# A third place for scores in the last unit, and reciprocals by block transposes instead of through DRAM

## The chip, the cores and the metric

The kernel runs on one core of one Trainium2 chip. The metric is the time of one execution in device microseconds (us); runs of the same kernel are summed up by their median. In the profile PE is TensorE (matrix products), DVE VectorE, ACT ScalarE, POOL GpSimd and SP the engine that issues most transfers (DMAs). Each engine works through its own instructions in the order in which the program lists them.

## The reference

Four batches of 1024 tokens, 512 features, go through three layers, each behind a layer norm and added to its input: a gated self-attention, a cross-attention on a context of 384 features, and a feed-forward layer of 64 small networks. The change lies in the cross-attention of the last batch:

```python
q = (query @ Wq + bq)...; k = (key_value @ Wk + bk)...; v = (key_value @ Wv + bv)...   # 16 heads of 32
attn = jnp.einsum('bhqd,bhkd->bhqk', q, k) * scale
attn = jax.nn.softmax(attn, axis=-1)
x = jnp.einsum('bhqk,bhkd->bqhd', attn, v).reshape(B, Nq, Cq)
return x @ Wo + bo
```

The feed-forward layer takes a scalar per network from the normalized tokens (s), passes it through 16 hidden units (h = relu(s * W1 + b1)), sums them with weights (g) and maps the 64 results back to 512 features. All is in float32.

## The kernel before

The work is cut into eight units: four batches in the first phase (self-attention), then four in the second (cross-attention). A unit has two halves of 512 queries, a half four groups g of four heads, a group eight steps kt, one for each 128 keys. So a unit has 64 steps; this text counts those of the last unit from 0 to 63.

A step (`step`, in `attention`) lists, in this order: what is due ahead of it; `scores`; what is due behind them; and `finish` of the step before, that is `times`. `scores` (L578) makes the transposed scores of two pairs of heads. Each pair has a place s of two PSUM banks; the pool `mps` has two such places, used in turn. ScalarE takes the exponential of a pair into e (L583, 128x1024); e has six buffers. `times` (L624) multiplies four heads' e by the values into the one bank av. In the last unit VectorE adds the e of steps 0 to 3 and of 4 to 7 of a group (L591, tiles sets). The sums over the keys come from TensorE with a column of ones: `by_ones` (L614) for steps 0 to 3, listed two steps after kt = 3, so in steps 5, 13, 21 and so on; `add_up` (L652) for the rest, in the second step of the next group. Both write the one bank sm, and only one row of each 32.

`normalize` evicts av into the tile both (ScalarE, L641) in the step after a group's last. Then the sums go on a way through DRAM, each part listed a few steps after the one before: `add_up` evicts sm (ScalarE, L653), writes four rows to DRAM and reads them back as 128 rows of 16 (L658, L660); three steps later `divide` takes the reciprocal (L689), two reductions for a check of the range (L690, L691), writes it to DRAM (L692) and reads each head's row back onto 32 partitions (L696, four transfers, tile recb); three more steps later `multiply` (L702) divides. The group of step 63 (`closing`) is done otherwise, in `settle`: its sums are made 32 columns wide and the reciprocal is taken from PSUM.

What else goes on is woven between the steps by `run`: `beside` gives a list of parts, each with a load in matmul blocks or 0, and `run` lists after each step as many as keep the shares of load equal. In the last unit the list of a half holds, of the half before: hidden units (L880 on ScalarE, then L884 and L886 on VectorE; hid has two buffers, so the hidden unit h waits for the VectorE instruction that has read h - 2), the output projection (L87 into a single bank f; steps 6 to 13 and 38 to 45), the output of the feed-forward layer of the half before that (L897, L903; steps 14 and 15, 46 and 47), layer norm (L290 to L299, L303), rows written to and read back from DRAM (L307, L312), the addition of the bias (L844), block transposes (L318) and the feed-forward input (L859; steps 24 and 56), which needs all four transposes. The pool `mpf` has two single banks f, which only these parts use. Parts without load, such as hidden units, fall into steps without matmuls of their own. [...]

The order of instructions on each engine is the order in which the code lists them.

Of the kernel before, what the change touches and what calls it, by code (L numbers as in the profile page):

```python
# [16 lines left out]
P = 128  # L17
# [46 lines left out]
def moderate_path(tc: tile.TileContext, a: dict, out: bass.AP, flag: bass.AP):  # L64
    nc = tc.nc
    x = a["x"]
    with ExitStack() as st:
# [9 lines left out]
        p3 = enter(tc.tile_pool(name="mp3", bufs=3))  # L77
        p4 = enter(tc.tile_pool(name="mp4", bufs=4))

        def bank():  # L80
            return pf.tile([P, HALF], F32, tag="f", name="f")

        def columns(to, lhsT, rhs, **flags):

# [268 lines left out]
        def pre(u):  # L353
# [194 lines left out]
                r[k] = [f(hf) for hf in range(2)]  # L548
            return r

        def attention(u, hf):

            ph, b = order[u]
# [13 lines left out]
            def closing(g):  # L567
                return (u, hf, g) == (len(order) - 1, 1, HG - 1)

            def scores(g, kt):  # L570
                q, k = me["q", hf], me["k"]
                es = []
                for i in range(2):
                    s = ps.tile([P, 2, HALF], F32, tag="s", name="s")
                    for j in range(2):
                        r = slice((2 * i + j) * DH, (2 * i + j + 1) * DH)
                        for m in range(0, P, 64):
                            nc.tensor.matmul(  # L578
                                s[m : m + 64, j, :], lhsT=k[r, g, kt * P + m : kt * P + m + 64], rhs=q[r, g, :],
                                start=True, stop=True,  # L580
                            )
                    e = p4.tile([P, 2, HALF], F32, tag="e", name="e", bufs=6)
                    nc.scalar.activation(e, s, AF.Exp, scale=SCALE)  # L583
                    es.append(e)
                me["e", kt] = es
                if fours:
                    if kt == 4 * (kt // 4) or closing(g) and kt == NT - 1:
                        return es
                    to = me["es"] = me["sets"][2 * (kt // 4) : 2 * (kt // 4) + 2]
                    for i in range(2):  # L590
                        nc.vector.tensor_tensor(to[i], me["e", kt - 1][i] if kt % 4 == 1 else to[i], es[i], ALU.add)  # L591
                    if kt == 3:
                        after(2, lambda: by_ones(g, to, True, False), behind=True)
                    return es
                for i in range(1 if shared else 2):
                    if kt == 1:
                        me.setdefault("es", {})[i] = p1.tile([P, 2, HALF], F32, tag=f"es{i}", name="es")
                        nc.vector.tensor_tensor(me["es"][i], me["e", 0][i], es[i], ALU.add)  # L598
                    elif kt > 1:
                        nc.vector.tensor_tensor(me["es"][i], me["es"][i], es[i], ALU.add)  # L600
                if ph == 0 and kt > 0:
                    if kt == 1:
                        me["eg"] = p1.tile([P, 2, HALF], F32, tag="es1", name="eg")
                    for h in range(2):
                        eg, gate = me["eg"][:, h, :], lambda t: me["sw"][:, t, HG * g + h, 1:2]
                        if kt == 1:
                            nc.vector.tensor_scalar(eg, me["e", 0][0][:, h, :], gate(0), None, ALU.mult)
                        nc.vector.scalar_tensor_tensor(eg, es[0][:, h, :], gate(kt), eg, ALU.mult, ALU.add)  # L608
                return es

            def by_ones(g, tiles, first, last):
                width = DH if closing(g) else 1
                for j in range(HG):
                    nc.tensor.matmul(  # L614
                        sm[j * DH : j * DH + width, :], lhsT=ones.to_broadcast([P, width]) if width > 1 else ones,
                        rhs=tiles[j // 2][:, j % 2, :], start=first, stop=last,
                    )
# [20 lines left out]
            def normalize(g):  # L638
                i = (u * 2 + hf) * HG + g
                both = p1.tile([P, 3, HALF], F32, tag="both", name="both")  # L640
                nc.scalar.copy(both[:, 0, :], av)  # L641
                if shared:
                    nc.scalar.copy(both[:, 1, :], sm)
                    added = [me["es"][0][:, 0, :], me["es"][0][:, 1, :], me["eg"][:, 0, :], me["eg"][:, 1, :]]
                else:
                    added = [me["es"][h // 2][:, h % 2, :] for h in range(HG)]
                after(1, lambda: add_up(g, i, both, added), behind=True)

            def add_up(g, i, both, added):

                for j, e in enumerate(added):
                    nc.tensor.matmul(sm[j * DH : j * DH + 1, :], lhsT=ones, rhs=e, start=not fours, stop=True)  # L652
                nc.scalar.copy(both[:, 2, :], sm)  # L653

                c, s1, s2 = cs_[i % 2], sum1_d[i % 4], sum2_d[i % 4]
                rows = both.rearrange("(j r) s q -> j r s q", r=DH)
                n = len(added)
# [13 lines left out]
                after(apart(g), lambda: divide(g, i, both, c))  # L671

            def divide(g, i, both, c):
                if shared:
# [71 lines left out]
        def post(u, hf):  # L746
# [24 lines left out]
            def project(t):  # L771
                def part(cs, to=None):
                    def f():
                        assert last or me["divided", hf] >= cs[-1]
                        if cs[0] == 0:
                            res["po"] = to() if to else bank()
                            res["po", t] = res["po"]
                        if last:
                            res["po"] = res["po", t]
                        for c in cs:  # L780
                            columns(
                                res["po"], me["q", hf][:, c, ts(t, P)], me["wo", hf][:, c, :],
                                start=(c == 0), stop=(c == NC - 1),
                            )
                        if cs[-1] < NC - 1:
                            return
                        r = res[t]
                        nc.vector.tensor_tensor(r, res["po"], r, ALU.add)  # L788
                        s6 = p2.tile([P, 6], F32, tag="bnst1", name="bnst1")
                        if t == 0:  # L790
                            res["mv"] = p2.tile([P, 4, 2], F32, tag="fmv", name="fmv")
                        nc.vector.bn_stats(s6, r)
                        nc.vector.bn_aggr(res["mv"][:, t, :], s6)
                        if ph == 0:
                            r2 = p2.tile([P, D], F32, tag="r2", name="r2")
                            nc.gpsimd.tensor_tensor(r2, r, bo_bc, ALU.add)  # L796
                            nc.sync.dma_start(x1b_d[b][4 * hf + t], r2)
                    return len(cs), f
                if last:
                    return [part([0, 1, 2], (lambda: ps.tile([P, 2, HALF], F32, tag="s", name="s")[:, 0, :]) if t > 1 else None), part([3])]  # L800
                return [part([c]) for c in range(4)]
# [146 lines left out]
                done = upto  # L948
            return [out + second[done:]]

        def run(main, items):

            parts = sum(items, [])
            total = sum(c for c, _ in parts)
            done = 0
            for n, f in enumerate(main):
                f()
                while parts and (done + parts[0][0] / 2 <= total * (n + 1) / len(main) or n == len(main) - 1):
                    c, f1 = parts.pop(0)
                    if f1:  # L960
                        f1()
                    done += c
# [95 lines left out]
        for u in range(n):  # L1058
            if u == 0:
                crossing.append(True)  # L1060
            for hf in range(2):
                run(attention(u, hf), beside(u, hf))
        tail = ending[0]
        sums, divide, look = settle(n - 1, 1, HG - 1)
        late.pop(0)()
# [676 lines left out]
```

## Time and profile before

| | |
|---|---|
| median of 3 runs | 2200.36 us (2195.76 to 2202.55) |
| the profiled execution | 2200.93 us, span 2199.1 us |
| PE, DVE, ACT busy | 2162.2, 1594.5, 1233.7 us |
| last unit, steps 0 to 63 | 1928.18 to 2146 us |
| exponential of a pair (L583) | 1.02 us, 1024 in all, 128 of them in the last unit |
| addition of a pair (L591) | 1.22 us |
| recb from DRAM (L696) | 64 KB each, 252 transfers |
| mean granted TensorE clock | 0.996 |

The span runs from the first instruction to the last. A line of a timeline gives the start, the length, the engine, the line of the code, the operation with output and input, and in brackets the idle time before it with the instruction that ended it. Successive matmuls of one line are drawn together as one block; a matmul is recorded twice (x16 is eight instructions). A block that waits inside is drawn longer, and its wait isn't idle time. A line of stretches gives, after the length, the busy time of PE, of its weight loads, of DVE, ACT and POOL with the number of instructions, then the granted clock, the DMA share and GB/s. A line of waits gives who waited for whom, the sum, how often and the longest.

### The profile page before, as it was taken

The page shows a single profiled execution, that of the slowest core. Times are in us where ns is not written, and L with a number is a line of the kernel's source. Part 1 is how long each engine was busy: PE and PEld are TensorE (multiplying, and loading weights), DVE is VectorE, ACT ScalarE, POOL GpSimd, SP SyncE. Part 2 cuts the span into 40 slices and gives each one's busy share as a digit, 9 for nine tenths or more (in the row PEclk, how much of TensorE's full clock was granted, in tenths as well). Part 3 has the DMA queues.
Part 4 walks back from the last instruction along what each step waited for, and adds up shares of the span by engine and source line. Part 5 has one row for each costly group of instructions (what it writes and reads, how often), then busy time and mean ns, then how long its engine had stood idle before and what let it go on. Part 6 is the DMA issues. An engine that isn't in the chain of part 4 may idle for free.

```text
span 2199.1 us, 52499 instructions
## 1 busy us (share of the span) xinstructions
PE 2162.2 (98%) x22482; PEld 545.9 (25%) x22482; DVE 1594.5 (73%) x2550; ACT 1233.7 (56%) x1482; POOL 81.7 (4%) x118
## 2 busy tenths in 40 slices
PE   8999999999999999999999999999999999999986
PEld 3322222222222222222222222222222222222222
DVE  4478675796757957567677676877777777878776
ACT  0155545555455554555656566675757666576663
POOL 1000000030210000000000000000000000000000
PEclk9999999999999999999999999999999999999998
DMA  4412123132231221211222132322233142212131
GB/s 141 130 62 55 63 95 106 29 88 66 97 104 32 82 69 47 69 56 42 70 85 90 45 90 67 79 73 56 69 84 112 50 103 69 64 36 76 62 88 41
DMA packets 152715, 161.63 MB, mean 73 GB/s; under 512 B 45628, under 2 KB 91324, under 8 KB 151320
## 3 DMA queue, kind: packets, MB, share of 16 engines
q1 hardware_dynamic: 148480, 156.08, 24.5%
q8 instruction: 178, 2.92, 0.6%
q0 software_dynamic: 2144, 0.98, 0.3%
q10 hardware_dynamic: 1848, 1.12, 0.2%
q14 instruction: 65, 0.53, 0.1%
HBM read 115.38 MB, written 42.71 MB: 72 GB/s over the span
## 4 chain that ended last, share of the span: by engine, by line
PE 92%; DVE 4%; issue 1%; DMA 1%; ACT 1%; SPq 0%; DVEq 0%; ACTq 0%
PE f L87 36%; PE s L578 25%; PE av L624 21%; PE sm L632 5%; PE sm L652 3%; DVE sets L591 1%; PE f L859 1%; ACT e L583 1%; DMA rec_d<-rec 0%; PE f L897 0%; DVE g L886 0%; PE sm L614 0%; DVE res L903 0%; PE f L471 0%; DMA recb<-rec_d 0%
## 5 line engine op out<-in xcount | busy, mean ns | idle before, releaser
L583 ACT ACTIVATE e<-s 128x1024 f32<-128x1024 f32 x1024 | 993.4, 1022 | 702.2 <-PE s L578 505.1
L600 DVE TENSOR_TENSOR es<-es,e 128x1024 f32<-128x1024 f32 x480 | 576.8, 1228 | 211.3 <-ACT e L583 209.6
L578 PE MATMUL s<-q,k 32*64 32x512 f32 x8192 | 610.6, 613 | 2.4 <-ACT e L583 0.9
L624 PE MATMUL av<-e,v 128*32 128x512 f32 x4096 | 544.8, 603 | 0.0
L87 PE MATMUL f<-xT,w 128*32 128x512 f32 x2816 | 333.7, 592 | 1.1 <-issue 1.1
L608 DVE SCALAR_TENSOR_TENSOR eg<-e,sw,eg 128x512 f32<-128x512 f32 x448 | 318.6, 747 | 2.3
L578 PEld LDWEIGHTS s<-q,k 32*64 32x64 f32 x8192 | 133.6, 129 | 448.7 <-ACT e L583 246.2
L87 PE MATMUL f<-w,q 128*32 128x512 f32 x1984 | 238.1, 592 | 0.0
L598 DVE TENSOR_TENSOR es<-e 128x1024 f32<-128x1024 f32 x80 | 95.8, 1223 | 192.9 <-ACT e L583 166.3
L624 PEld LDWEIGHTS av<-e,v 128*32 128x32 f32 x4096 | 88.0, 108 | 402.4 <-issue 399.1
L87 PEld LDWEIGHTS f<-xT,w 128*32 128x32 f32 x2816 | 92.1, 110 | 211.8 <-issue 206.4
L632 PE MATMUL sm<-e,sw 128*2 128x512 f32 x1024 | 133.3, 592 | 0.0
L87 PE MATMUL f<-w,xT 128*32 128x512 f32 x896 | 106.0, 592 | 0.6 <-DVE q L284 0.6
L87 PEld LDWEIGHTS f<-w,q 128*32 128x32 f32 x1984 | 64.5, 110 | 149.3 <-issue 142.8
L87 PE MATMUL f<-w,ctxT 128*32 128x512 f32 x768 | 92.6, 592 | 0.0
L87 PE MATMUL f<-ctxT,w 128*32 128x512 f32 x768 | 92.3, 592 | 0.0
L880 ACT ACTIVATE hid<-sT,units 128x256 f32<-128x256 f32 x128 | 76.6, 605 | 26.7 <-DVE g L886 22.9
L591 DVE TENSOR_TENSOR sets<-sets,e 128x1024 f32<-128x1024 f32 x62 | 73.1, 1221 | 9.3 <-ACT e L583 9.2
L796 POOL TENSOR_TENSOR r<-res,bo_bc 128x512 f32<-128x512 f32 x32 | 40.9, 1279 | 1041.9 <-DVE res L788 796.0
L886 DVE SCALAR_TENSOR_TENSOR g<-hid,units,g 128x256 f32<-128x256 f32 x120 | 57.6, 480 | 12.9 <-ACT hid L880 7.7
L591 DVE TENSOR_TENSOR sets<-e 128x1024 f32<-128x1024 f32 x32 | 37.8, 1221 | 30.6 <-ACT e L583 30.6
L652 PE MATMUL sm<-es,ones 128*1 128x512 f32 x320 | 57.8, 591 | 0.0
(243 smaller groups left out, 1108.1 us busy)
## 6 DMA issues: line engine op xcount, KB each, us to landing
recb<-rec_d SPq DMA_DIRECT2D x252, 64.0 KB
xT<-rows_d SPq DMA_DIRECT2D x60, 256.0 KB
rows_d<-r SPq DMA_DIRECT2D x60, 256.0 KB
w<-in_xattn_Wo SPq DMA_DIRECT2D x9, 1024.0 KB
w<-wout_d SPq DMA_DIRECT2D x8, 1024.0 KB
res<-in_x SPq DMA_DIRECT2D x32, 256.0 KB
x1b_d<-r SPq DMA_DIRECT2D x32, 256.0 KB
res<-x1b_d SPq DMA_DIRECT2D x32, 256.0 KB
```

Of the source, the lines that this page charges most:

```text
L87: nc.tensor.matmul(to[r], lhsT=lhsT[:, j, :] if len(lhsT.shape) == 3 else lhsT[:, r], rhs=rhs, **flags)
L578: nc.tensor.matmul(s[m : m + 64, j, :], lhsT=k[r, g, kt * P + m : kt * P + m + 64], rhs=q[r, g, :], start=True, stop=True,)
L583: nc.scalar.activation(e, s, AF.Exp, scale=SCALE)
L591: nc.vector.tensor_tensor(to[i], me["e", kt - 1][i] if kt % 4 == 1 else to[i], es[i], ALU.add)
L598: nc.vector.tensor_tensor(me["es"][i], me["e", 0][i], es[i], ALU.add)
L600: nc.vector.tensor_tensor(me["es"][i], me["es"][i], es[i], ALU.add)
L608: nc.vector.scalar_tensor_tensor(eg, es[0][:, h, :], gate(kt), eg, ALU.mult, ALU.add)
L624: nc.tensor.matmul(av[r, :], lhsT=me["v"][:, kt, HG * g + h, :], rhs=es[h // 2][:, h % 2, :], start=(kt == 0), stop=(kt == NT - 1),)
L632: nc.tensor.matmul(sm[j * DH : j * DH + sums, :], lhsT=me["sw"][:, t, HG * g + 2 + h, :], rhs=me["e", t][1][:, h, :], start=(kt == 1), sto ...
L652: nc.tensor.matmul(sm[j * DH : j * DH + 1, :], lhsT=ones, rhs=e, start=not fours, stop=True)
L880: nc.scalar.activation(hid, res["s"], AF.Relu, bias=units[:, 1, h : h + 1], scale=units[:, 0, h : h + 1])
L886: nc.vector.scalar_tensor_tensor(res["g"], res["hid"], units[:, 2, h - 1 : h], res["g"], ALU.mult, ALU.add)
```

## The change

Two parts, both in the last unit only.

The third place: `score_banks` gives a pair of scores either a place s, as before, or two single banks f. It gives banks when `run` says that neither the step's own parts nor those of the step before have a load (`spare`), no projection is open, and two pairs have been given s since a bank was last taken. A pair in banks has its exponential in two instructions of 512 columns. By the order of instructions this falls to 26 of the 128 pairs: in steps 1, 2, 4, 5; 17, 18, 20, 21, 23; 26, 27, 29, 30; 33, 34, 36, 37; 49, 50, 52, 53, 55; 58, 59, 61, 62.

The reciprocals of the groups with g > 0 (the closing one excepted; `quick`): both `by_ones` calls make their sums 32 columns wide, so all 128 rows of sm are written. One step after `add_up`, ahead of that step's scores (steps 18, 26, 34, 50, 58), `at_once` works on VectorE alone: `in_place` transposes sm by blocks of 32 by 32 into both, takes the reciprocal of one column of each block (128x16), transposes it back by blocks with each value repeated 32 times, makes the two reductions, and the multiplication follows. The eviction of sm and the seven transfers fall away for these five groups. Group 0 of each half keeps its way through DRAM.

```diff
+        def score_banks():
+
+            if spare[0] and not open_[0] and since[0] >= 2:
+                two = [bank(), bank()]
+                return two, [(slice(i, i + 1), b) for i, b in enumerate(two)]
+            since[0] += 1
+            s = ps.tile([P, 2, HALF], F32, tag="s", name="s")
+            return [s[:, i, :] for i in range(2)], [(slice(0, 2), s)]
...
+        def in_place(den, i, cols):
+
+            n = (cols.stop - cols.start) // NB
+            if cols.start == 0:
+                recs[i] = [
+                    p1.tile([P, HALF], F32, tag="recb", name="recb"), p2.tile([P, INNER], F32, tag="rec", name="rec")
+                ]
+            all_, rec = recs[i]
+            own = slice(cols.start // NB, cols.stop // NB)
+            nc.vector.transpose(den[:, cols], sm[:, cols])
+            column = den.rearrange("p (b j) -> p b j", j=NB)[:, own, 0]
+            nc.vector.reciprocal(rec[:, own], column)
+            nc.vector.transpose(all_[:, cols], rec[:, own].unsqueeze(2).to_broadcast([P, n, NB]))
+            if cols.stop == HALF:
+                nc.vector.tensor_reduce(marks[:, i : i + 1], den.rearrange("p (b j) -> p b j", j=NB)[:, :, 0], AX.X, ALU.add)
+                nc.vector.tensor_reduce(marks[:, NS + i : NS + i + 1], rec, AX.X, ALU.add)
+            return all_[:, cols]
...
+            def quick(g):
+                return u + 1 == len(order) and g > 0 and not closing(g)
...
-                    s = ps.tile([P, 2, HALF], F32, tag="s", name="s")
+                    two, reads = score_banks()
...
-                                s[m : m + 64, j, :], lhsT=k[r, g, kt * P + m : kt * P + m + 64], rhs=q[r, g, :],
+                                two[j][m : m + 64], lhsT=k[r, g, kt * P + m : kt * P + m + 64], rhs=q[r, g, :],
...
-                    nc.scalar.activation(e, s, AF.Exp, scale=SCALE)
+                    for h, s in reads:
+                        nc.scalar.activation(e[:, h, :] if len(reads) == 1 else e[:, h.start, :], s, AF.Exp, scale=SCALE)
...
-                width = DH if closing(g) else 1
+                width = DH if closing(g) or quick(g) else 1
...
-                for j, e in enumerate(added):
-                    nc.tensor.matmul(sm[j * DH : j * DH + 1, :], lhsT=ones, rhs=e, start=not fours, stop=True)
+                if fours:
+                    by_ones(g, added, False, True)
+                else:
+                    for j, e in enumerate(added):
+                        nc.tensor.matmul(sm[j * DH : j * DH + 1, :], lhsT=ones, rhs=e, start=True, stop=True)
+                if quick(g):
+                    after(1, lambda: at_once(g, i, both))
+                    return
                 nc.scalar.copy(both[:, 2, :], sm)
...
+            def at_once(g, i, both):
+                rec = in_place(both[:, 1, :], i, slice(0, HALF))
+                nc.vector.tensor_tensor(me["q", hf][:, g, :], both[:, 0, :], rec, ALU.mult)
+                me["divided", hf] = g
...
-        def run(main, items):
+        def run(main, items, shares=False):
...
+                coming, at = False, done
+                for c, f1 in parts:
+                    if at + c / 2 > total * (n + 1) / len(main):
+                        break
+                    coming, at = coming or bool(c and f1), at + c
+                spare[0] = shares and not (loaded or coming)
                 f()
+                spare[0], loaded = False, coming
...
-                run(attention(u, hf), beside(u, hf))
+                run(attention(u, hf), beside(u, hf), shares=u + 1 == n)
```

More of the change, by code (lines that the diff above doesn't have):

```diff
@@ L78, in moderate_path @@
         p4 = enter(tc.tile_pool(name="mp4", bufs=4))
+        spare = [False]
+        since = [0]
+        open_ = [0]
         def bank():
+            since[0] = 0
             return pf.tile([P, HALF], F32, tag="f", name="f")
+        def score_banks():
[5 more added lines that the diff above has]
+            return [s[:, i, :] for i in range(2)], [(slice(0, 2), s)]
         def columns(to, lhsT, rhs, **flags):
@@ L549, in pre @@
             return r
+        recs = {}
+        def in_place(den, i, cols):
[14 more added lines that the diff above has]
+            return all_[:, cols]
         def attention(u, hf):
@@ L645, in normalize @@
                 else:
-                    added = [me["es"][h // 2][:, h % 2, :] for h in range(HG)]
+                    added = me["es"] if fours else [me["es"][h // 2][:, h % 2, :] for h in range(HG)]
                 after(1, lambda: add_up(g, i, both, added), behind=True)
             def add_up(g, i, both, added):
-                for j, e in enumerate(added):
-                    nc.tensor.matmul(sm[j * DH : j * DH + 1, :], lhsT=ones, rhs=e, start=not fours, stop=True)
+                if fours:
[6 more added lines that the diff above has]
+                    return
                 nc.scalar.copy(both[:, 2, :], sm)
@@ L656, in add_up @@
                 rows = both.rearrange("(j r) s q -> j r s q", r=DH)
-                n = len(added)
+                n = HG
                 nc.sync.dma_start(s1[0:n], rows[0:n, 0, 2, :])
@@ L776, in f @@
                             res["po"] = to() if to else bank()
+                            open_[0] += 1
                             res["po", t] = res["po"]
@@ L786, in f @@
                             return
+                        open_[0] -= 1
                         r = res[t]
@@ L949, in weave @@
             return [out + second[done:]]
-        def run(main, items):
+        def run(main, items, shares=False):
             parts = sum(items, [])
             total = sum(c for c, _ in parts)
-            done = 0
+            done, loaded = 0, True
             for n, f in enumerate(main):
+                coming, at = False, done
[4 more added lines that the diff above has]
+                spare[0] = shares and not (loaded or coming)
                 f()
+                spare[0], loaded = False, coming
                 while parts and (done + parts[0][0] / 2 <= total * (n + 1) / len(main) or n == len(main) - 1):
```

## The prediction

> Steps are counted from 0 to 63 within the last unit (batch 3 of the second phase); step 0 starts its scores at 1928.18 us. A bare step is one that carries no projection, no output and no input matmuls beside its own. Before that unit the instruction streams of both kernels are the same, and after step 63 the tail is, so all of the change lies in 218 us.
>
> **What bounds the kernel now.** First the busy shares and the chain that ended last: TensorE has 98% and 92%, so the question is where in the last unit TensorE waits. Matmuls that wait inside a block are shown as a long block, so the lengths of blocks count, not idle time.
>
> ```profile
> PE 2162.2 (98%) x22482; PEld 545.9 (25%) x22482; DVE 1594.5 (73%) x2550; ACT 1233.7 (56%) x1482; POOL 81.7 (4%) x118
> PE 92%; DVE 4%; issue 1%; DMA 1%; ACT 1%; SPq 0%; DVEq 0%; ACTq 0%
> ```
>
> Then TensorE's timeline, steps 18 to 25:
>
> ```profile
> 1990.71 1.11 PE L578 MATMUL s<-q,k 32*64 32x512 f32 x16
> 1991.75 1.06 PE L624 MATMUL av<-e,v 128*32 128x512 f32 x8
> 1992.94 2.00 PE L578 MATMUL s<-q,k 32*64 32x512 f32 x16
> 1994.87 1.06 PE L624 MATMUL av<-e,v 128*32 128x512 f32 x8
> 1995.87 1.31 PE L578 MATMUL s<-q,k 32*64 32x512 f32 x16
> ...
> 2000.09 1.04 PE L614 MATMUL sm<-sets,ones 128*1 128x512 f32 x8
> ...
> 2013.14 3.51 PE L859 MATMUL f<-xn,win 128*32 128x256 f32 x28 [3.35 <-DVE xn L318]
> ```
>
> Scores of both pairs side by side take 1.04; where the second pair's place is still being read by the exponential they come one after the other, 2.00. A bare step without that stall lasts 1.04 + 1.00 = 2.04 (2.87 with four sums beside it, as step 25); these last 2.23 and 2.93 in turn, a stall of 0.54 each on average. Over all bare steps the stalls add up to some 22 us: 3.1 in steps 1 to 5, 4.2 in 17 to 23, 6.5 in 26 to 37, 5.0 in 49 to 55, 3.3 in 58 to 63.
>
> Next VectorE in the same steps, and the waits of the two stretches that end in L859 (1979 to 2014, 2086 to 2123):
>
> ```profile
> 2006.41 1.89 DVE L318 STREAM_TRANSPOSE xn<-xn 128x512 f32<-128x512 f32 x3
> 2009.51 0.69 DVE L702 TENSOR_TENSOR q<-both,recb 128x512 f32<-128x512 f32 x1 [1.21 <-DMA recb<-rec_d]
> 2010.12 2.35 DVE L591 TENSOR_TENSOR sets<-sets,e 128x1024 f32<-128x1024 f32 x2
> 2012.38 0.70 DVE L318 STREAM_TRANSPOSE xn<-xn 128x512 f32<-128x512 f32 x1
> ```
> ```profile
> 1979.99:2013.08 33.09, 29.38 (x268) 6.35 (x266) 31.01 (x49) 21.72 (x24) 0.00 (x0) 1.00 0.38 105
> 2086.83:2122.44 35.61, 30.22 (x268) 6.48 (x268) 31.20 (x49) 21.72 (x24) 0.00 (x0) 1.00 0.45 127
> ```
> ```profile
> DVE q L702 <- DMA recb<-rec_d: 2.3, 1, 2.3
> DVE r L303 <- DMA rows_d<-r: 1.4, 1, 1.4
> ```
>
> The third column of the stretches is VectorE: 31.01 of 33.09 and 31.20 of 35.61. From step 14 to the last transposition of xn, VectorE is the engine that sets the end; TensorE then waits 3.35 and 5.01 before L859. So in steps 16 to 24 and 48 to 56 the stalls of the scores cost nothing of their own: TensorE would only wait longer at L859. This is what decides the forecast.
>
> [...] L318 takes 0.67 to 0.70 for 512 elements, as L844 (an addition) does with 0.69. [...] granted clock 0.50 from 2013.0 to 2016.4 and from 2122.2 to 2125.6, after the two waits at L859, so L859's 28 records took 3.51 instead of the 1.7 that they would at the rate of 32 in 1.95 (step of 1922.55). [...] rec_d went out at 2000.03, the broadcasts that wait for its landing at 2004.93.
>
> **The change part by part.**
>
> *Reciprocals on the spot* (groups 1, 2, 3 of the first half, 1 and 2 of the second). Taken away per group: an eviction on ScalarE (L653, 0.60), seven transfers on SP's queue (sums out and in, reciprocals out, four broadcasts), the reciprocal and two reductions of steps 20, 28 and so on (L689 to L691: 1999.75 to 2000.12, 0.37 of VectorE). Added on VectorE, at the head of the step two after the group's last value matmul (steps 18, 26, 34, 50, 58): transposition 0.70 to its end, as the reciprocal needs it; reciprocal 0.25; transposition 0.60 by the spacing in L318 x3; two reductions 0.11 + 0.17: 1.83. The multiplication (0.69) only moves, from steps 23, 31 and so on to the same place. So 1.46 more VectorE per group. Bounds: an instruction reading PSUM is as fast as one reading SBUF here (L788 0.68, L844 0.69); the repeated-element input of the second transposition has no row: from 0.60 to twice that, 1.2; I take 0.60. The sums of 32 columns instead of one cost TensorE 0 (L614: 592 and 592 ns). SP's queue gets shorter; who waits on it there, x rows written and read back (L307, L312), keeps its place.
>
> In steps 16 to 24: 33.09 - 1.21 (wait for recb) + 1.46 = 33.34, a loss of 0.25 (a gain of 0.2 if the 0.45 us wait on an exponential in step 22 goes too). In 48 to 56: 35.61 - 2.32 - 0.19 (waits on recb and xn) + 1.46 = 34.56; the 1.40 on rows_d stays. Gain 1.05. What is late next is VectorE itself: the third addition of step 19 ended at 1999.24, and L614 of step 21 (the first half of the sums) at 2000.09 needs it. At_once puts it at about 1999.24 + 0.70 + 0.25 + 0.60 + 0.28 + 0.60 = 2001.7, while unstalled scores would bring TensorE there at about 1997. So TensorE's wait moves from L859 to L614, some 4.6 us in step 21 and the rest, 2 to 3 us, in step 24.
>
> *Third place*. By the order of instructions, 26 of 128 score pairs go to two single banks: 4 in steps 1 to 5, 5 in 17 to 23, 4 each in 26 to 30, 33 to 37 and 58 to 62, 5 in 49 to 55. Each splits one exponential of 1.02 into two of 512 columns. ScalarE's spacing is 0.92 for a whole one and 0.46 behind an eviction of 512 columns (1987.70 to 1988.16), so I take 0 extra; the upper bound is 0.17 each (two of 0.59 less 1.02), 4.4 in all. Nothing else waits for the banks, except step 17: its first pair needs L903's last read, 1987.6, so it gains nothing.
>
> Gain by stretch. Steps 1 to 7: ScalarE has work (exponentials and the 128x256 hid) for all but 0.8 of 14.91 us (busy 14.12), so at most 0.8 of the 3.1; part of it goes again in step 6, where hid waits for g behind VectorE's additions: 0.4. Steps 16 to 24 and 48 to 56: 0, the two results above stand. Steps 25 to 37: ScalarE busy 33.26 of 36.33 bounds the gain at 3.1. But at_once (steps 26 and 34) now stands in VectorE's queue ahead of L591 and of g (L886); g of step 26, at 2023.95, goes to 2023.95 - 0.19 + 1.83 = 2025.6, ends at 2026.1, hid behind it starts then instead of 2024.74, and the exponentials of step 28 come at 2026.6, not 2025.77. So the 2.2 of stalls in 26 to 29 is given back. Steps 30 and 31 gain 1.1, but step 32, the first of a half, has no third place and takes most of it; 34 to 37 repeat 26 to 29: 0.1 in all. Steps 57 to 63: the same up to 61, and 62 and 63 keep their gain: 0.5.
>
> Clock: the two half-speed periods (1.7 us lost in each) stay two[...]: 0, with 3.4 either way.
>
> Sum: 0.4 - 0.25 + 1.05 + 0.1 + 0.5 = 1.8. The profiled execution took 2200.93 (span 2199.1 and 1.8 around it), so 2199.1; it lies 0.57 above the median of the runs shown, so 2198.5 for the median.
>
> **Rivals.** *Faster*: VectorE keeps ahead. If TensorE doesn't meet L614 late (at_once fits into VectorE's waits), ScalarE's idle time is what is left to gain: 0.8 + 3.1 + 2.0 (20.53 less 18.54 in steps 57 to 63) in the outer stretches, 1.05 in 48 to 56, and both half-speed periods go, 3.4: 10.35 in all, 2190. For it: VectorE is idle for 7.8 of the 36.33 us of steps 25 to 37. Against it: that idle lies in other steps than those of at_once. *Slower*: the repeated-element transposition costs 1.2 or more, and TensorE halts at each of the five L614 (steps 21, 29, 37, 53, 61) long enough to lose its clock. Then 5 x 0.6 = 3.0 more on VectorE's path, three further half-speed periods of 1.7 = 5.1, and the halves of the exponentials up to 2: 10.1 - 1.8 = 8.3 more, 2209. [...] *Without effect*: the order shows the pairs and the transpositions in place, so that is out.
>
> **How the numbers follow.** Two executions of this kernel differ by up to 0.3% (2195.76 to 2202.55), 6.6 us, about what can be told from no change. The VectorE-bound case at 2198.5 has 0.60, its own range 2194.5 to 2203; faster at 2190 has 0.28; slower at 2209 has 0.12. Below 2193.8 counts as faster, above 2207 as slower, so the chances are these. The range takes in part of both: 2190.5 to 2205.5.
>
> **What would show it.** Right: scores of bare steps in blocks near 1.1 to 1.3 instead of 2.00, ScalarE with 52 exponentials of 512 columns; L614 of steps 21 and 53 waiting 4 us or more for L591, and L859 still waiting for L318; steps 14 to 25 as long as before within 1 us. Wrong: L859 without a wait, full clock through the unit, or transpositions from PSUM above 1 us. The forecast fails on the fast side if VectorE's additions run ahead of L614, on the slow side if clock drops appear in steps 25 to 37.

## The result, and the profile after

The changed kernel took 2206.73 us (median of 21 runs, 2199.09 to 2210.18) where the kernel before took 2199.75 (2194.98 to 2203.25): a ratio of 1.0029, interval 1.0020 to 1.0038, some 6.4 us slower. The forecast was 2198.5, no change, in a range of 2190.5 to 2205.5. The profiled execution of the changed kernel has a span of 2207.5 us and a mean granted clock of 0.991 (before: 2199.1 and 0.996).

The busy shares and the chain of waits of the changed kernel, to be set against those before:

```profile
PE 2163.8 (98%) x22482; PEld 551.7 (25%) x22482; DVE 1600.7 (73%) x2560; ACT 1232.8 (56%) x1503; POOL 82.5 (4%) x118
PE 89%; DVE 4%; DMA 2%; ACT 2%; issue 2%; SPq 0%; DVEq 0%; ACTq 0%
```

VectorE has 6.2 us more, TensorE 1.6: the work grew little. A record's length contains waiting, so the shares don't show where 8.4 us of span went. The steps do. Below are the lengths in us of the last unit's stretches, each from the first score of one step to that of another, and the half-speed windows (granted clock 0.50, 3.4 us each) that fall between steps 0 and 63. The other columns are experiments told further down.

| steps | before | after | before_filled_2 | all_filled_3 | third_multiply_only |
|---|---|---|---|---|---|
| 0 to 8 | 25.33 | 26.64 | 25.33 | 24.95 | 24.96 |
| 8 to 16 | 31.14 | 31.17 | 31.14 | 31.16 | 31.14 |
| 16 to 25 | 31.93 | 33.71 | 31.03 | 31.36 | 29.25 |
| 25 to 38 | 36.32 | 40.11 | 36.32 | 36.90 | 33.02 |
| 38 to 48 | 38.59 | 38.69 | 38.60 | 38.62 | 38.59 |
| 48 to 57 | 34.37 | 33.79 | 30.68 | 31.53 | 29.74 |
| 57 to 63 | 16.28 | 18.14 | 16.28 | 16.52 | 14.73 |
| sum | 214.0 | 222.3 | 209.4 | 211.0 | 201.4 |
| windows | 2 | 8 | 0 | 0 | 0 |

What lies after step 63 is as long as before (56.9 and 57.1). TensorE's timeline of the changed kernel, steps 18 to 25 again (start, length, engine, line, operation, count, and in brackets the idle time before and what ended it):

```profile
1993.89 1.28 PE L615 MATMUL s<-q,k 32*64 32x512 f32 x16
1995.10 1.07 PE L662 MATMUL av<-e,v 128*32 128x512 f32 x8
1996.10 0.66 PE L615 MATMUL f<-q,k 32*64 32x512 f32 x4
1996.12 0.66 PE L615 MATMUL s<-q,k 32*64 32x512 f32 x4
...
2003.57 2.20 PE L652 MATMUL sm<-sets,ones 128*32 128x512 f32 x6 [4.08 <-DVE sets L629]
2005.28 1.07 PE L662 MATMUL av<-e,v 128*32 128x512 f32 x2
...
2006.13 2.20 PE L662 MATMUL av<-e,v 128*32 128x512 f32 x6
...
2017.80 1.92 PE L910 MATMUL f<-xn,win 128*32 128x256 f32 x28 [1.60 <-DVE xn L332]
```

The score pairs now stand side by side (s and f interleaved). The halt has moved from the matmuls of the feed-forward input (3.35 before, now 1.60 at L910) to the first half of the sums, L652 (L614 before): 4.08. The matmuls after it run at half speed: six records of the sums take 2.20 where they take 1.76 at full speed (both with a wait for the second pair of the addition in them), and six records of the value matmuls behind them (L662) take 2.20, where eight take 1.07 in the steps before. VectorE in the same steps:

```profile
1995.95 1.16 DVE L317 TENSOR_SCALAR r<-res,fmv,yi 128x512 f32<-128x512 f32 x2 [1.48 <-DMA rows_d<-r]
1997.03 0.71 DVE L576 STREAM_TRANSPOSE both<-sm 128x512 f32<-128x512 f32 x1
1997.77 0.26 DVE L578 RECIPROCAL rec<-both 128x16 f32<-128x16 f32 x1
1998.06 0.71 DVE L579 STREAM_TRANSPOSE recb<-rec 128x512 f32<-128x512 f32 x1
1998.69 0.14 DVE L581 TENSOR_REDUCE marks<-both 128x1 f32<-128x16 f32 x1
1998.75 0.15 DVE L582 TENSOR_REDUCE marks<-rec 128x1 f32<-128x16 f32 x1
1998.83 0.68 DVE L719 TENSOR_TENSOR q<-both,recb 128x512 f32<-128x512 f32 x1
1999.42 2.35 DVE L629 TENSOR_TENSOR sets<-sets,e 128x1024 f32<-128x1024 f32 x2
2001.70 0.68 DVE L895 TENSOR_TENSOR res<-res,bout_bc 128x512 f32<-128x512 f32 x1
2002.30 2.35 DVE L629 TENSOR_TENSOR sets<-sets,e 128x1024 f32<-128x1024 f32 x2
```

The reciprocals on the spot stand ahead of the third addition, which L652 waits for: 1.80 us from 1997.03 to the multiplication, as forecast (1.83). New in this half is the wait of 1.48 for the rows: L317 needs the buffers of rows whose transfer to DRAM isn't through; before, only the second half waited for it (1.40). It isn't the change's alone, though: in a later trace of the kernel before with matmuls added elsewhere (before_filled below) the first half waited 1.3 too. The granted clock by stretch (us, then TensorE's, its weight loads', VectorE's, ScalarE's and GpSimd's busy time with the count, then the clock, the DMA share and GB/s):

```profile
1950.80:1954.20 3.40, 3.40 (x20) 0.87 (x16) 3.04 (x4) 1.30 (x2) 0.00 (x0) 0.50 0.02 5
...
2002.00:2008.80 6.80, 5.23 (x24) 1.26 (x32) 6.73 (x8) 0.96 (x2) 0.00 (x0) 0.50 1.13 252
2008.80:2032.70 23.90, 20.98 (x228) 5.19 (x216) 17.70 (x24) 16.90 (x24) 0.00 (x0) 1.00 0.25 90
2032.70:2036.10 3.40, 3.40 (x21) 0.48 (x16) 2.29 (x3) 2.64 (x5) 0.00 (x0) 0.50 0.00 0
...
2056.60:2060.00 3.40, 3.40 (x24) 0.67 (x24) 2.35 (x3) 2.79 (x5) 0.00 (x0) 0.50 0.00 0
2060.00:2114.60 54.60, 51.68 (x536) 12.26 (x528) 41.22 (x68) 32.91 (x40) 0.19 (x1) 1.00 0.20 68
2114.60:2121.40 6.80, 5.29 (x24) 1.26 (x32) 6.67 (x8) 0.90 (x2) 0.00 (x0) 0.50 0.73 121
...
2145.30:2148.70 3.40, 3.40 (x24) 0.76 (x24) 2.29 (x3) 2.63 (x5) 0.00 (x0) 0.50 0.00 0
```

Eight windows at half speed instead of two, two of them after each of the halts of steps 21 and 53, and one each after steps 7, 29, 37 and 61, where no halt of 3 us is seen.

### The profile page after: what moved, and what is told of

Same layout as the page of the kernel before. It is cut to its first block, busy times and chain, and to the rows that moved or that the text cites. A ratio compares the mean times of both kernels' runs of the same rounds, so it can differ in the third digit from the quotient of the medians.

```text
span 2207.5 us, 52467 instructions
## 1 busy us (share of the span) xinstructions
PE 2163.8 (98%) x22482; PEld 551.7 (25%) x22482; DVE 1600.7 (73%) x2560; ACT 1232.8 (56%) x1503; POOL 82.5 (4%) x118
## 4 chain that ended last, share of the span: by engine, by line
PE 89%; DVE 4%; DMA 2%; ACT 2%; issue 2%; SPq 0%; DVEq 0%; ACTq 0%
PE f L101 36%; PE s L615 23%; PE av L662 20%; PE sm L670 5%; PE sm L693 2%; ACT e L621 1%; DVE sets L629 1%; DMA w<-in_attn_Wo 1%; PE sm L652 1%; DVE g L937 1%; PE f L910 0%; PE f L948 0%; DVE es L638 0%; ACT hid L931 0%; DMA res<-x1b_d 0%
## 5 line engine op out<-in xcount | busy, mean ns | idle before, releaser
L621 ACT ACTIVATE e<-s 128x1024 f32<-128x1024 f32 x998 | 969.7, 1022 | 710.7 <-PE s L615 502.2
L615 PE MATMUL s<-q,k 32*64 32x512 f32 x7984 | 596.4, 614 | 4.8 <-ACT e L621 4.5
L662 PE MATMUL av<-e,v 128*32 128x512 f32 x4096 | 552.2, 608 | 0.3 <-ACT e L621 0.3
L101 PE MATMUL f<-xT,w 128*32 128x512 f32 x2816 | 333.7, 592 | 0.4 <-PE f L101 0.4
L101 PE MATMUL f<-w,q 128*32 128x512 f32 x1984 | 240.0, 595 | 0.0
L662 PEld LDWEIGHTS av<-e,v 128*32 128x32 f32 x4096 | 89.5, 109 | 406.1 <-issue 401.4
L101 PEld LDWEIGHTS f<-xT,w 128*32 128x32 f32 x2816 | 92.4, 110 | 210.8 <-issue 203.8
L101 PE MATMUL f<-w,xT 128*32 128x512 f32 x896 | 106.0, 592 | 0.6 <-DVE q L298 0.6
L101 PEld LDWEIGHTS f<-w,q 128*32 128x32 f32 x1984 | 66.4, 111 | 149.0 <-issue 141.8
L101 PE MATMUL f<-w,ctxT 128*32 128x512 f32 x768 | 92.6, 592 | 0.0
L101 PE MATMUL f<-ctxT,w 128*32 128x512 f32 x768 | 92.3, 592 | 0.0
```

Source lines behind the costliest of these rows:

```text
L101: nc.tensor.matmul(to[r], lhsT=lhsT[:, j, :] if len(lhsT.shape) == 3 else lhsT[:, r], rhs=rhs, **flags)
L615: nc.tensor.matmul(two[j][m : m + 64], lhsT=k[r, g, kt * P + m : kt * P + m + 64], rhs=q[r, g, :], start=True, stop=True,)
L621: nc.scalar.activation(e[:, h, :] if len(reads) == 1 else e[:, h.start, :], s, AF.Exp, scale=SCALE)
L662: nc.tensor.matmul(av[r, :], lhsT=me["v"][:, kt, HG * g + h, :], rhs=es[h // 2][:, h % 2, :], start=(kt == 0), stop=(kt == NT - 1),)
```

## The experiments

Theory: the two parts disturb each other. The third place brings TensorE sooner to the places where it needs VectorE, the reciprocals on the spot make VectorE later there; TensorE halts, and the halts cost it the clock. Rivals: one of the parts costs time by itself; or VectorE's queue sets the stretches and the clock is a by-product. Ratios are to the kernel before, run on the same chip.

**One part alone.** The third place without the reciprocals:

```
-                return u + 1 == len(order) and g > 0 and not closing(g)
+                return False
```

> Only the third place for scores; the reciprocals of all groups go through DRAM as before. Theory A (the reciprocals on the spot stand ahead of VectorE's third addition, TensorE halts at the first half of the sums and loses its clock; the third place is innocent): faster than before, by 2 to 5 us (0.9977 to 0.9991), with half-speed periods of 3.4 us only before L859, as before, and one in step 7. Theory B (the third place itself is the loss: split exponentials, and TensorE runs sooner into halts that cost it the clock): slower than before, 3 us or more (1.0014 up). Theory C (each alone is harmless, only both together make the halts long enough): within 2 us of before or faster.

2193.64 us, ratio 0.9976 (0.9967 to 0.9985). The reciprocals without the third place:

```
-                run(attention(u, hf), beside(u, hf), shares=u + 1 == n)
+                run(attention(u, hf), beside(u, hf))
```

> Only the reciprocals on the spot; scores always in the two places. Theory A: slower than before by 3 to 6 us, halts at the sums of steps 21 and 53 of some 2 to 3 us, with half-speed periods there. Theory B: faster than before by 1 to 3 us, since the waits on recb are gone. Theory C: within 2 us of before; halts at L614 of 1 to 2 us that leave the clock at full speed in the last unit but for one period at most.

2200.88 us, ratio 1.0012 (1.0005 to 1.0019). So the third place gains some 5.3 us, the reciprocals lose 2.6, and both together lose 6.4: 9 us more than the sum of the two. Step 16 doesn't start at the same time in these traces, so count from its start. TensorE begins the scores of step 21 after 13.53 us in spot_only, 12.16 in third_only and 12.19 in the changed kernel, and the sums that need VectorE's third addition start after 15.89, 15.19 and 17.62 (before: 13.50 and 15.43, without a halt). With the reciprocals alone TensorE comes later and VectorE is less late; with the third place alone TensorE comes early, but so does VectorE:

```profile
2002.47 1.76 PE L652 MATMUL sm<-sets,ones 128*32 128x512 f32 x6 [0.36 <-DVE sets L629]
```
```profile
1999.43 1.85 PE L652 MATMUL sm<-sets,ones 128*1 128x512 f32 x6 [1.68 <-DVE sets L629]
```

The first line is of spot_only, the second of third_only: halts of 0.36 and 1.68 where both parts have 4.08. In step 53 the halts are 1.70, 1.33 and 4.12. That the third place costs time by itself falls.

The clock is only part of these 9 us. The mean granted clock over all runs is 0.9957 in third_only and 0.9966 in spot_only, where the kernel before has 0.9960 on that chip; the changed kernel has 0.9930 against 0.9956 (after_again below). So both together lose 0.0029 more than the sum of the two, which at 1.5 to 1.8 us per 0.001 (an estimate, from the table of clocks below) makes some 4 to 5 us. The rest would be the order of the work on VectorE; no run here separates it.

**TensorE kept busy in the halts.** Both parts, and four products that nobody uses ahead of L652 in steps 21 and 53:

```
+                            if g == 2:
+                                for _ in range(4):
+                                    nc.tensor.matmul(sm, lhsT=ident, rhs=me["k"][:, 0, 0:HALF], start=True, stop=True)
                             by_ones(g, to, True, False)
```

> The changed kernel, and four products of 128x512 into the bank of the sums just ahead of the first half of the sums in steps 21 and 53, where TensorE halts 4.1 us; the sums overwrite them, so the output is the same. It keeps TensorE busy for 3.4 us of the halt without shortening it. If the lost clock is exposed: the two half-speed periods of 6.8 us are gone, and the kernel is 3 to 6 us faster than the changed one (about 1.0005 to before). If the halt alone is the loss (VectorE sets the end there), it is within 1 us of the changed one (1.0025 to 1.0033).

2199.72 us, ratio 1.0005 (0.9997 to 1.0012). Work was added and the kernel became some 3.5 to 5 us faster than the changed one (ratio 1.0029, and 1.0021 when it was measured again); the four products take 3.70 us ahead of the sums of step 21 (L634), and the four windows after the two halts are gone from the trace. What is left of windows in the last unit came after steps 29 and 61 (2029.8 and 2139.1). One more product there, between the two score pairs:

```
+                    if fours and (g, kt, i) == (3, 5, 1):
+                        nc.tensor.matmul(sm, lhsT=ident, rhs=k[:, 0, 0:HALF], start=True, stop=True)
```

> As both_filled, and between the two score pairs of steps 29 and 61 one more product of 512 columns with 128 weights (0.93 us in both_filled), so that TensorE works through most of the halt of 1.32 us there. It computes nothing that is used. Theory (a halt of 1.0 to 1.3 us is enough to lose the clock [...]): the half-speed windows after steps 29 and 61 go (2029.8 and 2139.1 in both_filled), 1.7 us each; 2196.3 where both_filled has 2199.7, and about 3 us under the kernel before. Rival (those steps are set by ScalarE and VectorE, whatever TensorE's clock): as both_filled, 2199.7.

2199.17 us, ratio 1.0002 (0.9994 to 1.0011). In its trace both windows are gone and steps 25 to 32 and 57 to 63 take 19.37 and 16.53 us, 1.6 us less each than in both_filled (21.01 and 18.16), as expected, and two later traces of this kernel (all_filled_again, all_filled_3) have the same lengths within 0.01. The median did not follow. The profiled execution of both_filled was one of its slowest (2203.28), and its mean clock over all runs is 0.9966 against 0.9968 here, so most of its runs seem not to have lost these windows. The gain is shown in the traces and not in the medians.

**Reciprocals two steps later.**

```
-                    after(1, lambda: at_once(g, i, both))
+                    after(3, lambda: at_once(g, i, both))
```

> The changed kernel with the reciprocals on the spot listed two steps later (steps 20, 28, 36, 52, 60), ahead of a step without an addition, so behind the third addition instead of ahead of it. Theory A: the halts at L614 shrink from 4.1 to about 1 us, fewer half-speed periods, and 4 to 8 us faster than the changed kernel (0.9993 to 1.0010 to before). Theory B: no better than the changed kernel (1.0029).

2196.17 us, ratio 0.9986 (0.9979 to 0.9993): the same instructions as in the changed kernel, and some 9.5 us less by the ratios. Steps 25 to 38 take 33.8 us instead of 40.1. Of these 6.3 us some 3.2 are the two half-speed windows after steps 29 and 37, which this trace doesn't have (all_filled_3, without windows too, takes 36.9); the rest goes with the reciprocals no longer standing ahead of g, which hid waits for: ScalarE's longest wait for g in steps 25 to 31 is 0.25 us here and 1.94 in the changed kernel. In steps 21 and 53 the halt stays; now the sums wait for the transposition that reads the old ones:

```profile
2001.44 1.93 PE L652 MATMUL sm<-sets,ones 128*32 128x512 f32 x8 [3.68 <-DVE both L576]
```

**The sums two steps later**, in the whole change (sums_later), in the third place alone (third_sums_later) and together with later reciprocals (spot_sums_later):

```
-                        after(2, lambda: by_ones(g, to, True, False), behind=True)
+                        after(4, lambda: by_ones(g, to, True, False), behind=True)
```

> The whole change, but the first half of each group's sums comes two steps later (steps 7, 15 and so on instead of 5, 13), so that TensorE meets it after VectorE's additions. Theory (the two parts disturb each other because TensorE halts at the first half of the sums and then loses its clock): the halts of 4.1 us in steps 21 and 53 go, the 6.8 us at half speed that followed each go or shrink to one window before the output matmuls; steps 16 to 25 take some 31 us instead of 33.7, and the whole about 2197 where the kernel before has 2199.5. Rival (TensorE's halts are only moved, to the output matmuls which wait for the last transposition, with the same clock lost there): as after, about 2206.

2203.08 us, ratio 1.0014 (1.0008 to 1.0021): a miss, between the theory's 2197 and the rival's 2206. The halts at L652 are gone, and the same time turns up at L910:

```profile
2011.01 0.62 PE L910 MATMUL f<-xn,win 128*32 128x256 f32 x4 [0.89 <-DVE xn L332]
2014.47 3.23 PE L910 MATMUL f<-xn,win 128*32 128x256 f32 x28 [2.83 <-DVE xn L332]
```

VectorE's queue sets the end of steps 16 to 25 (32.7 us here), as the rival said; only the number of windows in the last unit falls, from eight to six, and the one after step 29 stays.

> Third place without reciprocals on the spot, and the first half of the sums two steps later. Theory: without the spot reciprocals VectorE is early enough, so L652 hardly halts TensorE in third_only (2193.6); moving the sums takes away what is left of it in steps 21 and 53: 2192 to 2194 where before has 2199.5. Rival (the third place's own stall at L652 was worth something): 2190 or less.

2194.99 us, ratio 0.9978 (0.9971 to 0.9984): as third_only.

> The whole change with the spot reciprocals two steps later and the first half of the sums two steps later as well. Theory: both meetings of TensorE and VectorE are taken out, the second half-speed window that spot_later still had after steps 21 and 53 goes, 1.7 us each: about 2193 (spot_later 2196.2). Rival (what bounds steps 16 to 25 is VectorE's queue alone, wherever TensorE waits): as spot_later, 2196.

2197.98 us, ratio 0.9994 (0.9985 to 1.0002): not better than spot_later. Moving the sums moves the halt. This kernel also shows that the clock alone doesn't set the time: its mean granted clock over all runs, 0.9929, is that of the changed kernel (0.9930), and yet it is some 6 us faster by the ratios (0.9994 and 1.0021).

**The multiplication of group 1 one step later**, without the reciprocals on the spot, once with the later sums and once without:

```
-                return 2 if u + 1 < len(order) else 3
+                return 2 if u + 1 < len(order) else 4 if g == 1 else 3
```

> As third_sums_later, and the multiplication of group 1 comes one step later, behind the transpositions of xn in VectorE's queue, so that its wait for the broadcast reciprocals (0.7 to 2.3 us in steps 23 and 55) delays nothing. Theory (VectorE sets the end of steps 16 to 25 and 48 to 57): 1 to 2 us less than third_sums_later, about 2191.5. Rival (the transpositions then only wait earlier for rows from DRAM): the same as third_sums_later.

> Third place without reciprocals on the spot, the first half of the sums in its old place, and the multiplication of group 1 one step later. Theory (the gain of third_multiply_later over third_only comes from the multiplication, which no longer holds VectorE in steps 23 and 55): about 2192.5, as third_multiply_later. Rival (it needs the later sums as well): as third_only, 2193.6.

2192.6 us, ratio 0.9968 (0.9956 to 0.9981), and 2189.75 us (five runs), ratio 0.9965 (0.9951 to 0.9978). Some 7 us faster than the kernel before, the two can't be told apart; the second has five runs, and its interval meets that of third_only (0.9967 to 0.9985), so that the gain over third_only isn't shown by the medians. In the trace VectorE no longer waits for the broadcast reciprocals ahead of the transpositions of xn; in third_multiply_only:

```profile
2007.69 1.89 DVE L332 STREAM_TRANSPOSE xn<-xn 128x512 f32<-128x512 f32 x3
2009.51 2.32 DVE L629 TENSOR_TENSOR sets<-sets,e 128x1024 f32<-128x1024 f32 x2
2011.74 0.70 DVE L332 STREAM_TRANSPOSE xn<-xn 128x512 f32<-128x512 f32 x1
2012.37 0.65 DVE L751 TENSOR_TENSOR q<-both,recb 128x512 f32<-128x512 f32 x1
```

TensorE's two halts there are 1.36 (L652) and 1.85 (L910), and the last unit has no half-speed window. What the reciprocals on the spot were to take away, the wait for a transfer, goes by an order of two instructions, with no work added.

**The kernel before with its halts filled.** What the change is worth where the clock is full on both sides needs a kernel before without half-speed windows:

```
+                if u + 2 == n:
+                    for _ in range(3 + hf):
+                        nc.tensor.matmul(ss, lhsT=ident, rhs=S[n - 1]["k"][:, 0, 0:HALF], start=True, stop=True)
```

> The kernel before with three products (first half) and four (second half) of 128 weights by 512 columns, 0.93 us each, put just ahead of L859 of steps 24 and 56, where TensorE otherwise halts for 3.35 and 5.01 us; they compute nothing that is used. Theory (the clock is what those halts cost TensorE after they end): both half-speed windows of the last unit go, some 1.5 us each, about 2196.5 where the kernel before has 2199.5; and against all_filled it shows what the whole change costs with the clock full on both sides: 1 to 2 us more. Rival (the change gains 1.8 us where the clock is equal, as forecast): all_filled lies below before_filled.

> all_filled once more, on the same chip as before_filled. Theory: 1 to 2 us above before_filled. Rival (the change gains 1.8 us where the clock is equal): 1.8 us below it.

2198.65 us, ratio 1.0000 (0.9992 to 1.0008), and 2198.0 us, ratio 0.9998 (0.9989 to 1.0007). Inconclusive: the edit was misplaced. Three of the products stood two steps ahead of step 0, where TensorE doesn't halt, and delayed step 0 by 2.1 us; step 56 had none. With the condition `(u, hf) in ((n - 2, 1), (n - 1, 0))` and `range(4 - hf)` they stand in steps 24 and 56 alone:

> The kernel before with three idle products (0.93 us each) ahead of L859 in step 24 and four in step 56, and none elsewhere (before_filled had three ahead of step 0, which cost 2.1 us there, and none in step 56). Theory: both half-speed windows of the last unit go and the products hide in halts of 3.35 and 5.01 us: about 2197, 1.5 to 3 us under the kernel before. Rival (the windows lost there cost nothing, because VectorE sets the end of these stretches): as the kernel before.

> all_filled on the chip of before_filled_2: what the whole change costs where the clock is full in the last unit on both sides. Theory (VectorE's 1.46 us in the stretch to the output matmuls and the new wait for the rows show): 1 to 2 us above before_filled_2. Rival (the forecast's sum holds at equal clock): 1.8 us below it.

> The changed kernel once more, on the same chip. Theory (the loss is the clock): its runs lie on one line with those of the kernel before when span is set against granted clock: at a clock of 0.996 some 2198 as before, 1.9 us more per 0.001 of clock lost. Rival (work was added): at equal clock its spans are longer by 5 us or more.

On one chip: before_filled_2 2196.54 us (eight runs), ratio 0.9973 (0.9963 to 0.9984); all_filled_3 2198.91, ratio 0.9990 (0.9982 to 0.9998); the changed kernel again 2206.41, ratio 1.0021 (1.0013 to 1.0029). TensorE in before_filled_2 at L862 (L859 before), and in all_filled_3 at L659 (L652 of the changed kernel):

```profile
2009.39 2.84 PE L858 MATMUL f<-k,ident 128*128 128x512 f32 x6
2012.16 0.63 PE L862 MATMUL f<-xn,win 128*32 128x256 f32 x4
2013.92 1.92 PE L862 MATMUL f<-xn,win 128*32 128x256 f32 x28 [1.13 <-DVE xn L318]
```
```profile
1998.27 3.70 PE L636 MATMUL sm<-k,ident 128*128 128x512 f32 x8
2002.03 1.76 PE L659 MATMUL sm<-sets,ones 128*32 128x512 f32 x6
```

With the clock kept, L862's 28 records take 1.92 and not 3.51, and the sums' six 1.76 and not 2.20. In steps 21 and 53 of all_filled_3 the added products hold the sums back by 0.06 us at most: so much earlier VectorE's addition ends. all_filled_3 is 2.4 us above before_filled_2, 1.7 us in the two traces: the change loses with a full clock too; the rival, that the forecast's sum holds there (1.8 us below), falls. How much it loses is less sure: before_filled_2 has eight runs, and the two intervals touch.

The spans of all runs on that chip can also be set against their mean granted clock. Number of runs and mean span in us:

| clock | before | after_again |
|---|---|---|
| 0.991 | | 2, 2205.2 |
| 0.992 | | 8, 2205.0 |
| 0.993 | | 5, 2203.1 |
| 0.994 | 7, 2200.8 | 3, 2203.5 |
| 0.995 | 8, 2199.8 | 1, 2200.3 |
| 0.996 | 17, 2198.8 | 1, 2197.7 |
| 0.997 | 6, 2194.4 | 1, 2196.6 |

At the same clock the two kernels lie within -1.1 and +2.7 us of each other, with one to three runs of the changed kernel in each of these rows; the means, 2198.7 at 0.9956 and 2203.4 at 0.9930, differ by 4.7. A line through the points of either kernel falls by 1.8 and 1.5 us per 0.001 of clock, which makes, by estimate, 3.9 to 4.7 of the 4.7 the clock's. That a lower clock is cause and not only company is shown by both_filled, where keeping TensorE busy brought most of the time back (2199.72 us against 2206.73).

## Why the prediction was wrong, step by step

Of the 222.3 - 214.0 = 8.3 us by which the last unit grew in the profiled execution, 222.3 - 211.0 = 11.3 are the eight windows, against 214.0 - 209.4 = 4.6 that went with the two before (part of these 4.6 is a shorter wait for transfers in that execution): 6.7 of clock. The rest, 1.6, is the change at full clock. The forecast had 0 and -1.8. The profiled execution of the changed kernel (2209.35) is one of its slowest; that of after_again, in the same kernel, lost seven windows.

- **Clock: the step that failed, and the larger error.** "The two half-speed periods stay two ... 0." They became eight. Two things were wrong in it. It counted no clock lost after short halts; but half speed also followed halts of 0.69 to 1.32 us, in steps 7, 29, 37 and 61 (last section). And the long halts, 4.08 and 4.12 where 4.6 was forecast, were followed by two windows each (granted clock 0.50 from 2002.0 to 2008.8 and from 2114.6 to 2121.4), where L859's waits of 3.35 and 5.01 before were followed by one each. TensorE was busy for 0.90 of the 3.41 us ahead of step 21's first window and for 1.84 of the 3.41 of that window; before, for none of the 3.41 us from 2118.71 to 2122.12 and for 3.04 of the 3.41 that followed at half speed. Why a second window came wasn't tested. The slow rival came nearest: it had three more windows, and clock drops in steps 25 to 37 as the sign of failing on the slow side, which came. But it looked for them at L614, tied them to a dear transposition and put them at 0.12; in steps 29, 37 and 61 they came behind score pairs that waited for ScalarE.
- **Where the stalls go: right.** The halt moved from L859 to L614's place and left 1.60 at L859's; bare steps fell to 2.04 and 2.20; steps 0 to 8 gained 0.38 with the clock full (0.4 forecast).
- **Prices: right.** Transpositions 0.71 from PSUM and 0.71 with the repeated input, at_once 1.80 us to the multiplication (1.83); the split exponentials cost next to nothing, 1.06 to 1.10 for two halves against 1.02 for a whole one. Two readings are slightly off: L859's 28 records take 1.92 at full clock (before_filled_2), not 1.7, and 2195.76 to 2202.55 are 6.8 us, not 6.6. Neither changes the forecast.
- **Steps 16 to 24: right in size, +0.33 (0.25 forecast), by luck in part.** The wait for recb that goes was 1.90 in before_filled_2, not 1.21; and the wait of 1.48 for the rows came in, which the forecast had only in the second half and which differs from execution to execution.
- **Steps 48 to 56: wrong, +0.85 instead of -1.05.** The sum counted the wait for recb of the one profiled execution, 2.32, as if it were always there. In step 55 it was 0.54 in before_filled_2 and none in before_filled. 0.54 - 1.46 is a loss of 0.92, near what was measured.
- **Steps 25 to 37 and 57 to 63: wrong by 0.7 each,** +0.58 and +0.24 instead of -0.1 and -0.5. The way was forecast: at_once ahead of g, g ahead of hid, hid ahead of the exponentials of step 28. It reached further than put down, and it needs no third place: in spot_only, where scores are never split, steps 25 to 37 take 38.80 and 57 to 63 17.63 us, 2.5 and 1.35 more than before, and ScalarE waits 1.75 for g. ScalarE in the changed kernel:

```profile
2026.94 1.10 ACT L621 ACTIVATE e<-f 128x512 f32<-128x512 f32 x2
2029.98 0.60 ACT L931 ACTIVATE hid<-sT,units 128x256 f32<-128x256 f32 x1 [1.94 <-DVE g L937]
2030.48 1.92 ACT L621 ACTIVATE e<-s 128x1024 f32<-128x1024 f32 x2
```

With the exponentials of steps 26 and 27 sooner by the third place, ScalarE waited 1.94 for g, and TensorE 1.32 for ScalarE in step 29; half speed followed (2032.7 to 2036.1), and went when all_filled put one more product there. The third place alone took 2.8 us off steps 25 to 37 (33.51 in third_only); the reciprocals took that away.

What stays open: the share of the clock in the median is known to some 2 us only (3.9 to 4.7 of 4.7 by the table of clocks, 2.7 of 5.1 by the medians of the filled kernels). How the 9 us of the two parts together divide between clock and VectorE's order is an estimate only, and removing the wait for the rows by more buffers was not tried.

## What to carry to other kernels

Where one engine is 98% busy and its clock falls after halts, as TensorE's did here (to 0.50 for 3.4 us), ask of each change not only how long the engine waits but into how many halts its waiting is split and what follows each: a halt that moves or splits can cost more at half speed than it saves in time (here eight windows instead of two, by the traces 6.7 us). Two edits that are tried one by one can add up to a loss when one makes the consumer early and the other the producer late; run each alone. A wait for a transfer read from one execution is a sample, not a price (recb in step 55: 2.32, 0.54 and none in three executions): reorder the instruction behind other work before paying with new instructions to take it away.

## What the runs showed of the hardware

The clock fell after stretches in which TensorE worked for most of the time. The 3.4 us ahead of four of the drops to 0.50, in the changed kernel (us, TensorE's busy time and matmul records, clock, DMA share, GB/s):

```profile
1947.39:1950.80 3.41, 2.40 (x24) 0.99 0.00 0
...
2029.29:2032.70 3.41, 2.09 (x20) 1.00 0.01 2
2053.19:2056.60 3.41, 2.72 (x20) 1.00 0.02 5
2141.89:2145.30 3.41, 2.37 (x20) 1.00 0.00 0
```

TensorE was busy for 2.09 to 2.72 us of each, with a halt of 0.69 to 1.32 us in it.

The length of the halt alone doesn't decide it. The halt of step 7, first in the profiled execution, then in that of after_again:

```profile
1948.44 2.00 PE L615 MATMUL s<-q,k 32*64 32x512 f32 x16 [1.01 <-ACT e L621]
...
1951.72 3.12 PE L101 MATMUL f<-w,q 128*32 128x512 f32 x16
```
```profile
1948.20 2.00 PE L615 MATMUL s<-q,k 32*64 32x512 f32 x16 [1.01 <-ACT e L621]
...
1951.01 1.90 PE L101 MATMUL f<-w,q 128*32 128x512 f32 x16
```

The same halt of 1.01 us, followed by half speed (3.12 for L101's block) in one and not in the other (1.90). The halt of step 37, in the changed kernel and in both_filled:

```profile
2054.89 1.56 PE L615 MATMUL f<-q,k 32*64 32x512 f32 x8 [0.69 <-ACT e L621]
2056.38 1.75 PE L652 MATMUL sm<-sets,ones 128*1 128x512 f32 x8
2057.88 1.95 PE L662 MATMUL av<-e,v 128*32 128x512 f32 x8
```
```profile
2052.85 1.56 PE L615 MATMUL f<-q,k 32*64 32x512 f32 x8 [0.69 <-ACT e L621]
2054.34 1.04 PE L657 MATMUL sm<-sets,ones 128*1 128x512 f32 x8
2055.20 1.04 PE L667 MATMUL av<-e,v 128*32 128x512 f32 x8
```

Again one halt, 0.69 us, and eight records of the sums in 1.75 us after it in one, in 1.04 in the other. Nor does the busy time alone decide it. In third_multiply_only TensorE was busy for 1.56 of 3.41 us, less than ahead of the four drops above, and no half speed followed in the last unit:

```profile
2110.91:2114.32 3.41, 1.56 (x22) 1.00 0.00 0
```

What sets these apart isn't shown, and no run tested it. What is shown is that executions of one kernel differ in it: the profiled execution of the changed kernel has eight half-speed windows in the last unit and that of after_again seven, and over the runs of after_again the mean span goes from 2205.2 us at a mean clock of 0.991 to 2196.6 at 0.997.
